# Token tiles of 128 rows with a last one of 113 instead of five of 125, rows of tokens at a pitch of 640 columns

## The chip, the core and the metric

The kernel runs on one core of a Trainium2 chip. The metric is the device time of one execution in microseconds (us); the times shown are medians of several runs. The core has five engines that work side by side from queues of their own: TensorE (PE, with its weight loads shown apart as PEld), VectorE (DVE), ScalarE (ACT), GpSimd (POOL) and SyncE (SP, which here only issues DMAs). The data moves through 16 DMA engines.

## The reference

The input is x, 625 tokens (graph nodes) by 1024 features in float32, and 20000 edges (src, dst), sorted by dst. The kernel computes

```
xn  = layernorm(x)
deg = number of edges into each node;  inv = 1 / max(deg, 1)
h   = relu(xn @ Ws0 + (segment_sum(xn[src], dst) * inv) @ Wn0 + b0)
g   = h @ Ws1 + (segment_sum(h[src], dst) * inv) @ Wn1 + b1
q,k,v = xn @ Wq, xn @ Wk, xn @ Wv           # 16 heads of 64
q   = softmax(q over features) / 8;  k = softmax(k over tokens)
m   = (q @ (k.T @ v) per head) @ Wo + bo
x   = x + g + m
y   = layernorm(x);  top 2 of 8 experts by softmax(y @ router_w)
x   = x + sum over the two of p_e * (silu(y @ w1[e]) @ w2[e])
        + sigmoid(y @ sgw) * ((silu(gate) * up) @ shared_down),  gate,up = y @ shared_gate_up
```

All weight matrices are 1024 x 1024 in float32 (shared_gate_up is 1024 x 2048). The result is x, 625 x 1024 float32.

## The kernel before

Every float32 operand is split into a high part in fp32r (`split`, L75: ACT casts, DVE or POOL subtracts) and a low part, and each product is three fp32r matmuls: high by high, high by low, low by high. Weights come as 512 KB pieces through one ordered `Stream` (SP issues the loads at L100, three buffers deep, six in the expert stage) and are split on arrival.

Tokens are cut into NT = 5 tiles of T = 125 rows. Two layouts occur. In the natural one the tokens lie on the partitions (`slot_n`: 128 x 5 x 1024), and one tile fills 125 of them. In the turned one the features lie on the partitions and the tokens along the row (`slot_t`: 128 x 8 x 626, so a row of tokens has a pitch of NP = 626 columns).

There are two kinds of products. `ws_tile` and `keys_step` keep the weights in the array (128 x 128) and stream the tokens past them in two stretches of about 313 columns. `ts_half` keeps one tile of tokens in the array (128 x 125) and streams 512 columns of weights past it:

```python
for t in range(NT):
    c = slice(t * T, (t + 1) * T)
    for k in range(2):
        kt = 2 * u + k
        ...
        nc.tensor.matmul(accs[t][:T, :], xh[:, kt, c], wh[:, k, :], start=f, stop=False)
        nc.tensor.matmul(accs[t][:T, :], xh[:, kt, c], wl[:, k, :], start=False, stop=False)
        nc.tensor.matmul(accs[t][:T, :], xl[:, kt, c], wh[:, k, :], start=False, stop=s)
```

One call is 120 matmuls (4 pieces of weights, 5 tiles, 2 k, 3 products), and it is called 14 times: queries (psq), values (psv), the output projection (pso), the neighbour products of both graph layers (psg, twice), the self product of the second (psx) and the shared expert's down projection (psz), two halves each. Within one piece of weights the tile is the outer loop, so six matmuls of one tile stand together.

The order of the stages:

1. Start. SP issues the loads of x tiles 0 and 1 (`load_x`, L282), the edges (L287), the first piece of Wk, x tiles 2 to 4, and then the stream. Each x tile is normalised in place (DVE statistics at L229, ACT or DVE at L305 and L307), turned on PE (L257) and split into xnh and xnl. ACT casts the edges (L313) and PE turns them (L317) so that 125 edges lie on the partitions.
2. Keys and the first self product: `keys_step` for 16 column blocks. The first three blocks are worked in two passes: first tokens 0 to 249 (x tiles 0 and 1), then, when tiles 2 to 4 are turned, the remaining columns.
3. Beside stage 2, the adjacency counts: DVE makes pairs of one-hot rows from 125 edges each (L432, L433), and PE multiplies them (L455). Each count is packed as one of five base-32 fields of a float, a field for each of the five token tiles of src. The inputs of the one-hots come from a chain on POOL (L414 to L424). The last link, `first_col`, is read by DVE into registers, ten times (`value_load`, L457). Then the counts are unpacked into ath, five tiles of tokens by 626 columns.
4. Queries, values, attention, output projection; graph layers 1 and 2; the second layer norm.
5. The shared expert's gate and up products, the router, a scatter of the tokens to expert rows (indirect DMA on POOL, L1050), eight experts with fixed capacities, a gather of the expert rows (indirect DMA on POOL, L1206).
6. End. The shared down projection (psz); for each of two halves and five tiles DVE adds the last product (L1217) and SP stores 125 rows of 512 columns (L1218).

A scheduler places the instructions of an engine's queue by priorities and estimated times, except where `keep_in_program_order` or `high_priority` binds them. The places of the one-hots and of the register loads in the DVE queue are its choice.

Of the kernel before, what the change touches and what calls it, by code (L numbers as in the profile page):

```python
# [20 lines left out]
T = 125  # L21
NT = N // T
NP = N + 1
D = 1024
KT = D // 128
E = 20000
NG = 10
CH = E // (T * NG)
# [19 lines left out]

@with_exitstack
def gps_layer(ctx: ExitStack, tc: tile.TileContext, x, src, dst,  # L50
# [12 lines left out]
    def slot_t(name, dt=F32R):  # L63
        t = big.tile([128, KT, NP], dt, name=name, tag="big")
        return t
# [109 lines left out]
    def ts_half(xh, xl, accs, first=True, last=True, step=None):  # L175
        for u in range(4):
            wh, wl = st.next()
            for t in range(NT):
                c = slice(t * T, (t + 1) * T)
                for k in range(2):  # L180
                    kt = 2 * u + k
                    f = first and kt == 0
                    s = last and kt == KT - 1
                    nc.tensor.matmul(accs[t][:T, :], xh[:, kt, c], wh[:, k, :], start=f, stop=False)  # L184
                    nc.tensor.matmul(accs[t][:T, :], xh[:, kt, c], wl[:, k, :], start=False, stop=False)  # L185
                    nc.tensor.matmul(accs[t][:T, :], xl[:, kt, c], wh[:, k, :], start=False, stop=s)  # L186
            if step:
                step(u)
# [35 lines left out]
    def stats(xt, mv, half=None, order=None):  # L224

        st6 = half if half is not None else small.tile([128, 2, 6], F32, name="bnst")
        for h in range(2):
            if half is None:
                order(nc.vector.bn_stats(st6[:T, h, :], xt[:, h * 512:(h + 1) * 512]))  # L229
        nc.vector.bn_aggr(mv, st6[:T])  # L230
# [21 lines left out]
    def to_t(nat, t, hi, lo, order=None):  # L252
        for g in range(2):
            ps = bank("pst").rearrange("p (a b) -> p a b", b=128)
            for k in range(4):
                kt = 4 * g + k
                tr = nc.tensor.transpose(ps[:, k, :T], nat[:, kt], ident[:T, :T])  # L257
                if order:
                    order(tr)
            done = split(ps[:, :, :T], hi[:, 4 * g:4 * g + 4, t * T:(t + 1) * T],  # L260
                         lo[:, 4 * g:4 * g + 4, t * T:(t + 1) * T])
# [15 lines left out]
    ei = big.tile([128, 2, CH * T], I32, name="ei", tag="big")  # L277
# [3 lines left out]
    def load_x(t):  # L281
        keep(nc.sync.dma_start(xts[:T, t, :], x[t * T:(t + 1) * T, :]))  # L282
# [8 lines left out]

    lnv = const.tile([128, NT, 2], F32, name="lnv")
    lnt = const.tile([128, 3, NT], F32, name="lnt")

    def first_stats(t):
        stats(xts[:T, t, :], lnv[:T, t, :], order=keep)

    def first_norm(a, b):
# [3 lines left out]
        for t in range(a, b):  # L302
            xt = xts[:T, t, :]
            if t % 2:
                nc.scalar.activation(xt, xt, AF.Identity, bias=z[:, t:t + 1], scale=y[:, t:t + 1])  # L305
            else:
                nc.vector.tensor_scalar(xt, xt, lnv[:T, t, 0:1], y[:, t:t + 1], op0=ALU.subtract, op1=ALU.mult)  # L307

    def first_turn(t, order=None):
        return to_t(xts[:T, t, :].rearrange("p (k c) -> p k c", c=128), t, xnh, xnl, order)  # L310

    edges = big.tile([128, 2, CH * T], F32, name="edges", tag="big")
# [3 lines left out]
    for i in range(2 * CH):  # L316
        nc.tensor.transpose(pse[:T, i, :], edges[:NG, i // CH, (i % CH) * T:(i % CH + 1) * T], ident[:NG, :NG])  # L317
    nc.scalar.copy(edt[:T], pse[:T])
    esrc, edst = edt[:T, :CH, :], edt[:T, CH:, :]
# [23 lines left out]
    def keys_back(o):  # L343
        ke = kbuf[:, o % 3, :N]
        for t0, n in ((0, 3), (3, 2)):
            ps = bank("pskt").rearrange("p (a b) -> p a b", b=128)
            for t in range(n):
                nc.tensor.transpose(ps[:T, t, :], ke[:, (t0 + t) * T:(t0 + t + 1) * T], ident)
            nc.scalar.copy(knat[:T, t0:t0 + n, o * 128:(o + 1) * 128], ps[:T, :n, :])
# [64 lines left out]
    keep(nc.gpsimd.tensor_scalar(field[:T], esrc, 1.0 / T, -0.496, op0=ALU.mult, op1=ALU.add))  # L414
    keep(nc.gpsimd.tensor_scalar(field[:T], field[:T], MAGIC, None, op0=ALU.add))
    keep(nc.gpsimd.tensor_scalar(field[:T], field[:T], MAGIC, None, op0=ALU.subtract))
    keep(nc.gpsimd.tensor_scalar(srow[:T], field[:T], -float(T), None, op0=ALU.mult))
    keep(nc.gpsimd.tensor_add(srow[:T], srow[:T], esrc))

    keep(nc.gpsimd.tensor_scalar(unit[:T], field[:T], BITS * 2.0 ** 23, (127.0 - 2 * BITS) * 2.0 ** 23,  # L420
                                 op0=ALU.mult, op1=ALU.add))
    keep(nc.gpsimd.tensor_sub(edst, edst, first_dst[:T, None, :].to_broadcast([T, CH, NG])))
# [8 lines left out]
    def one_hot(h, i, g):  # L431
        nc.vector.tensor_scalar(h[:T, :WIN], iota[:T, :WIN], edst[:, i, g:g + 1], None, op0=ALU.is_equal)  # L432
        nc.vector.tensor_scalar(h[:T, WIN:], iota[:T, :WIN], srow[:T, i, g:g + 1],  # L433
                                unit[:T, i, g:g + 1].bitcast(F32), op0=ALU.is_equal, op1=ALU.mult)
# [10 lines left out]
    def count_chunks(n):  # L445
        for _ in range(n):
# [7 lines left out]
            h = hot[:T, c % RING, :]  # L454
# [26 lines left out]
    ath = atp.tile([128, NT, NP], F32R, name="ath")  # L481
    degs = const.tile([128, 5, NT], F32, name="degs")
    two = const.tile([128, 2], F32R, name="two")
    nc.vector.memset(two.bitcast(F32), 1.0)

    def unpack():
        for s in range(NT - 1, 0, -1):
# [3 lines left out]
            nc.vector.tensor_scalar(ath[:T, s, :], part[:T], MAGIC, None, op0=ALU.subtract)  # L491
            nc.vector.scalar_tensor_tensor(packed[:T, :NP], ath[:T, s, :].bitcast(F32), -step, packed[:T, :NP],
                                           op0=ALU.mult, op1=ALU.add)
        nc.scalar.activation(ath[:T, 0, :], packed[:T, :NP], AF.Identity, scale=2.0 ** (2 * BITS))
        nc.vector.reduce_max(degs[:T, 4, 1:2], ath[:T, NT - 1, :].bitcast(F32), axis=AX.X)
# [5 lines left out]
    def degrees():  # L501
        ps = bank("psdg")
        for t in range(NT):
            for s in range(NT):
                nc.tensor.matmul(ps[:T, 2 * t:2 * t + 2], ath[:T, s, t * T:(t + 1) * T], two[:T],
                                 start=s == 0, stop=s == NT - 1)
        nc.vector.tensor_copy(degs[:T, 0, :], ps[:T, :2 * NT].rearrange("p (t k) -> p t k", k=2)[:, :, 0])
# [20 lines left out]
    def recount():  # L528
# [4 lines left out]
        nc.vector.tensor_tensor(edst, edst, first_dst[:T, None, :].to_broadcast([T, CH, NG]), op=ALU.add)  # L533
        nc.vector.tensor_scalar(field[:T], esrc, float(HW), None, op0=ALU.is_ge)
        nc.vector.scalar_tensor_tensor(esrc, field[:T], -float(HW), esrc, op0=ALU.mult, op1=ALU.add)
        nc.vector.tensor_scalar(field[:T], field[:T], 4095.0, 1.0, op0=ALU.mult, op1=ALU.add)
        with tc.For_i(0, NT, 1) as r:
            nc.vector.memset(acc, 0.0)
            with tc.For_i(0, NG, 1) as g:
                ps = bank("pa")  # L540
                for i in range(CH):
                    h = tmp.tile([128, WIN + HW + 1], F16, name="hrare", tag="tmp")
                    nc.vector.tensor_scalar(h[:T, :WIN], iota[:T, :WIN], edst[:, i, ds(g, 1)], None, op0=ALU.is_equal)
                    nc.vector.tensor_scalar(h[:T, WIN:WIN + HW], iota[:T, :HW], esrc[:, i, ds(g, 1)],
                                            field[:T, i, ds(g, 1)], op0=ALU.is_equal, op1=ALU.mult)
                    nc.tensor.matmul(ps[:, :HW], h[:T, :WIN], h[:T, WIN:WIN + HW], start=i == 0, stop=i == CH - 1)
# [7 lines left out]
        for j in range(NT):  # L554
            aj = tmp.tile([128, NP], F32, name="aj", tag="tmp")
            nc.gpsimd.dma_start(aj[:T], ard[j * T:(j + 1) * T, :])
            for s0, n in ((0, 3), (3, 2)):
                ps = bank("psat").rearrange("p (a b) -> p a b", b=128)
                for s in range(n):
                    nc.tensor.transpose(ps[:T, s, :T], aj[:T, (s0 + s) * T:(s0 + s + 1) * T], ident[:T, :T])  # L560
                c = slice(j * T, (j + 1) * T)
                al = tmp.tile([128, 3, T], F32R, name="al", tag="tmp")
                split(ps[:T, :n, :T], ath[:T, s0:s0 + n, c], al[:T, :n, :])
                for s in range(n):
                    nc.gpsimd.dma_start(atd[(s0 + s) * T:(s0 + s + 1) * T, c], al[:T, s, :])
        for t in range(NT):
            pt = bank("psdt")
            for s in range(NT):
                al = tmp.tile([128, T + 1], F32R, name="al", tag="tmp")
                nc.gpsimd.dma_start(al[:T, :T], atd[s * T:(s + 1) * T, t * T:(t + 1) * T])  # L570
                nc.tensor.matmul(pt[:T, :2], ath[:T, s, t * T:(t + 1) * T], two[:T], start=s == 0, stop=False)
                nc.tensor.matmul(pt[:T, :2], al[:T, :T], two[:T], start=False, stop=s == NT - 1)
            nc.vector.tensor_copy(degs[:T, 0, t:t + 1], pt[:T, 0:1])
        inverse_degrees()

    def low_part(s):
        al = tmp.tile([128, NP], F32R, name="al", tag="tmp")
        nc.gpsimd.dma_start(al[:T, :N], atd[s * T:(s + 1) * T, :N])
        nc.vector.memset(al[:T, N:NP].bitcast(F32), 0.0)
# [3 lines left out]
    def inverse(t0, n):  # L583
        ps = bank("psd").rearrange("p (a b) -> p a b", b=128)
        for t in range(n):
            nc.tensor.transpose(ps[:, t, :T], degs[:T, 2, t0 + t:t0 + t + 1].to_broadcast([T, 128]), ident[:T, :T])
        nc.scalar.copy(dinv[:, t0 * T:(t0 + n) * T].rearrange("p (a b) -> p a b", b=T), ps[:, :n, :T])
# [22 lines left out]
    def queries_back(half, t, q):  # L610
        qf = q.rearrange("p h d -> p (h d)")
        pt = bank("psqt").rearrange("p (a b) -> p a b", b=128)
        for k in range(4):
            nc.tensor.transpose(pt[:, k, :T], qf[:T, k * 128:(k + 1) * 128], ident[:T, :T])
        nc.scalar.copy(qt[:, 4 * half:4 * half + 4, t * T:(t + 1) * T], pt[:, :, :T])

    def queries(half, accs):
        for t in range(NT):
            ps = accs[t][:T, :].rearrange("p (h d) -> p h d", d=64)
# [629 lines left out]
```

## Time and profile before

| | us |
|---|---|
| median of 3 runs | 1074.67 (1072.81 to 1074.84) |
| the profiled execution's own time | 1069.91 |
| its span from first to last instruction | 1068.3 |
| PE busy in the span | 1021.3 |
| DVE / ACT / POOL busy | 600.7 / 395.4 / 172.0 |
| mean granted TensorE clock | 0.984 |
| matmuls of 128 x 125 by 512 columns, one group of 80, busy time | 31.5 to 32.6 |
| DMA moved | 164.30 MB, mean 154 GB/s |

The profile gives each engine's busy time, the groups of instructions, what each wait was ended by, and the timeline. A matmul's own duration overlaps its successor's, so the pace of PE is read from the distance between starts, not from durations. The DMA share is the mean busy share of all 16 DMA engines, so one engine that is always busy counts 1/16.

### The profile page before, as it was taken

The page shows a single profiled execution, that of the slowest core. Times are in us where ns is not written, and L with a number is a line of the kernel's source. Part 1 is how long each engine was busy: PE and PEld are TensorE (multiplying, and loading weights), DVE is VectorE, ACT ScalarE, POOL GpSimd, SP SyncE. Part 2 cuts the span into 40 slices and gives each one's busy share as a digit, 9 for nine tenths or more (in the row PEclk, how much of TensorE's full clock was granted, in tenths as well). Part 3 has the DMA queues.
Part 4 walks back from the last instruction along what each step waited for, and adds up shares of the span by engine and source line. Part 5 has one row for each costly group of instructions (what it writes and reads, how often), then busy time and mean ns, then how long its engine had stood idle before and what let it go on. Part 6 is the DMA issues. An engine that isn't in the chain of part 4 may idle for free. (4 is left out here: it accounts for less than half of the span.)

```text
span 1068.3 us, 14752 instructions
## 1 busy us (share of the span) xinstructions
PE 1021.3 (96%) x5571; PEld 872.7 (82%) x5571; DVE 600.7 (56%) x1188; ACT 395.4 (37%) x577; POOL 172.0 (16%) x204
## 2 busy tenths in 40 slices
PE   4789999999999999999999999999999989999986
PEld 2689999888887777977777899998878777887765
DVE  2599953545253322722326636258686788877481
ACT  2333423222231122222113432246656576776410
POOL 2322001211015300010000104123030033200310
PEclk7899999999999999999999999999999999999999
DMA  5222134666233522052221125866967898888961
GB/s 134 87 60 61 41 96 143 216 231 223 62 119 115 165 88 79 23 154 79 73 68 38 31 60 131 237 193 193 277 233 231 263 300 282 281 286 269 305 152 73
DMA packets 116344, 164.30 MB, mean 154 GB/s; under 512 B 11079, under 2 KB 68431, under 8 KB 116262
## 3 DMA queue, kind: packets, MB, share of 16 engines
q1 hardware_dynamic: 97606, 118.54, 35.2%
q0 software_dynamic: 18656, 44.71, 14.1%
q8 instruction: 47, 0.77, 0.3%
q14 instruction: 35, 0.29, 0.1%
HBM read 133.04 MB, written 30.16 MB: 153 GB/s over the span
## 5 line engine op out<-in xcount | busy, mean ns | idle before, releaser
L75 DVE TENSOR_TENSOR wlo<-wraw,whi 128x1024 fp32r<-128x1024 f32 x140 | 177.9, 1271 | 267.4 <-ACT whi L75 266.4
L75 ACT CAST whi<-wraw 128x1024 fp32r<-128x1024 f32 x149 | 156.3, 1049 | 306.2 <-PE psg L186 68.2
L1089 PE MATMUL pse<-xs,whi 128*128 128x448 f32 (+1 forms) x384 | 108.9, 357 | 0.0
L75 DVE TENSOR_TENSOR wlo<-wmore,whi 128x1024 fp32r<-128x1024 f32 x67 | 86.9, 1297 | 23.5 <-ACT whi L75 22.5
L1085 PE MATMUL pse<-xs,wlo 128*128 128x224 f32 (+1 forms) x384 | 89.6, 254 | 0.6 <-DVE wlo L75 0.6
L75 ACT CAST whi<-wmore 128x1024 fp32r<-128x1024 f32 x67 | 70.3, 1049 | 51.6 <-PE psz L186 22.4
L376 PE MATMUL psk<-xnh,whi 128*128 128x314 f32 (+3 forms) x256 | 83.9, 328 | 4.8 <-DVE xnl L75 4.5
L377 PE MATMUL psk<-xnl,whi 128*128 128x314 f32 (+3 forms) x256 | 79.6, 311 | 1.0 <-DVE xnl L75 0.9
L378 PE MATMUL psk<-xnh,wlo 128*128 128x314 f32 (+3 forms) x256 | 79.5, 310 | 0.0
L1085 PEld LDWEIGHTS pse<-xs,wlo 128*128 128x128 f32 x384 | 72.0, 190 | 1.7 <-DVE wlo L75 0.8
L1141 PE MATMUL psy<-wlo,he 128*128 128x512 f32 (+1 forms) x176 | 70.0, 397 | 3.3 <-DVE wlo L75 3.0
L1089 PEld LDWEIGHTS pse<-xs,whi 128*128 128x128 f32 x384 | 69.0, 189 | 2.4
L1140 PE MATMUL psy<-whi,he 128*128 128x512 f32 (+1 forms) x176 | 69.5, 395 | 0.0
L1142 PE MATMUL psy<-whi,he 128*128 128x512 f32 (+1 forms) x176 | 69.0, 392 | 0.0
L433 DVE TENSOR_SCALAR hot<-iota,srow,unit 125x128 f16<-125x128 f16 x160 | 56.6, 354 | 0.0
L376 PEld LDWEIGHTS psk<-xnh,whi 128*128 128x128 f32 x256 | 49.4, 193 | 5.8 <-DVE xnl L75 5.0
L75 POOL TENSOR_TENSOR xs<-raw,xs 128x512 fp32r<-128x512 f32 (+2 forms) x24 | 34.4, 1455 | 104.2 <-ACT xs L75 83.4
L377 PEld LDWEIGHTS psk<-xnl,whi 128*128 128x128 f32 x256 | 49.3, 193 | 1.4 <-DVE xnl L75 1.4
L378 PEld LDWEIGHTS psk<-xnh,wlo 128*128 128x128 f32 x256 | 49.0, 192 | 0.1
L432 DVE TENSOR_SCALAR hot<-iota,edt 125x128 f16<-125x128 f16 x160 | 43.7, 273 | 7.9 <-issue 7.9
L1141 PEld LDWEIGHTS psy<-wlo,he 128*128 128x128 f32 (+1 forms) x176 | 31.8, 180 | 14.8 <-DVE wlo L75 6.7
L1140 PEld LDWEIGHTS psy<-whi,he 128*128 128x128 f32 (+1 forms) x176 | 31.9, 181 | 10.1
(337 smaller groups left out, 2385.0 us busy)
## 6 DMA issues: line engine op xcount, KB each, us to landing
wraw<-in_L_ffn_w_dram SPq DMA_DIRECT2D x65, 512.0 KB
wmore<-in_L_ffn_w_dram SPq DMA_DIRECT2D x63, 512.0 KB
xsd<-zt POOLq DMA_DIRECT2D x9, 1024.0 KB, 6.2
wraw<-in_L_gnn_W_self_dram SPq DMA_DIRECT2D x16, 512.0 KB
wraw<-in_L_gnn_W_neigh_dram SPq DMA_DIRECT2D x16, 512.0 KB
wraw<-_ffn_shared_gate_up_dram SPq DMA_DIRECT2D x16, 512.0 KB
wraw<-in_L_mix_Wk_dram SPq DMA_DIRECT2D x8, 512.0 KB
wraw<-in_L_mix_Wq_dram SPq DMA_DIRECT2D x8, 512.0 KB
```

What stands on the lines that cost most here:

```text
L75: return (nc.scalar.copy(hi, srcap), (eng or nc.vector).tensor_sub(lo, srcap, hi.bitcast(F32)))
L376: nc.tensor.matmul(ps[:, :n], wh[:, kt, :], xnh[:, kt, c], start=kt == 0, stop=False)
L377: nc.tensor.matmul(ps[:, :n], wh[:, kt, :], xnl[:, kt, c], start=False, stop=False)
L378: nc.tensor.matmul(ps[:, :n], wl[:, kt, :], xnh[:, kt, c], start=False, stop=kt == KT - 1)
L432: nc.vector.tensor_scalar(h[:T, :WIN], iota[:T, :WIN], edst[:, i, g:g + 1], None, op0=ALU.is_equal)
L433: nc.vector.tensor_scalar(h[:T, WIN:], iota[:T, :WIN], srow[:T, i, g:g + 1], unit[:T, i, g:g + 1].bitcast(F32), op0=ALU.is_equal, op1=ALU. ...
L1085: nc.tensor.matmul(ps[a][:, :n], wl[:, k, c], xs[:, kt, 0, :], start=False, stop=False)
L1089: nc.tensor.matmul(ps[a][:, :2 * n], wh[:, k, c], xs[:, kt], start=kt == 0, stop=kt == KT - 1)
L1140: nc.tensor.matmul(acc, h(kt, 0), wh[:, k, :], start=kt == 0, stop=False)
L1141: nc.tensor.matmul(acc, h(kt, 0), wl[:, k, :], start=False, stop=False)
L1142: nc.tensor.matmul(acc, h(kt, 1), wh[:, k, :], start=False, stop=kt == KT - 1)
```

## The change

T becomes 128, so the tiles have 128, 128, 128, 128 and 113 rows. `rows(t)` and `cols(t)` give the partitions and columns of tile t, and every place that used `[:T]` and `t * T` uses them. The edges keep their own 125 (ET). Rows of tokens in the turned layout, and those of ath, get a pitch of XP = 640 columns instead of 626. Loads of x and stores of the result go through `pieces(t)`, which cuts the last tile into 112 rows and 1 row, so SP issues one load more and two stores more. The two stretches of the shared products become 384 and 242 columns (they were 374 and 252), and those of the first three key blocks 256 and 370 (they were 250 and 376). Three small memsets (lnv, degs, lgt) fill the rows that the last tile doesn't write, and the degrees are copied in two instructions. The branch for rare graphs (`recount`) is changed too; it isn't taken with these inputs.

```diff
 N = 625
-T = 125
-NT = N // T
+T = 128
+NT = -(-N // T)
...
+XP = NT * T
...
-CH = E // (T * NG)
+ET = 125
+CH = E // (ET * NG)
...
+def rows(t):
+
+    return slice(0, min(T, N - t * T))
+
+
+def cols(t):
+
+    return slice(t * T, min((t + 1) * T, N))
+
+
+def pieces(t):
+
+    n = min(T, N - t * T)
+    m = n // 16 * 16
+    return [(slice(t * T + a, t * T + b), slice(a, b)) for a, b in ((0, m), (m, n)) if b > a]
...
-        t = big.tile([128, KT, NP], dt, name=name, tag="big")
+        t = big.tile([128, KT, XP], dt, name=name, tag="big")
...
-                c = slice(t * T, (t + 1) * T)
+                c, acc = cols(t), accs[t][rows(t), :]
...
-                    nc.tensor.matmul(accs[t][:T, :], xh[:, kt, c], wh[:, k, :], start=f, stop=False)
...
+                    nc.tensor.matmul(acc, xh[:, kt, c], wh[:, k, :], start=f, stop=False)
...
-                tr = nc.tensor.transpose(ps[:, k, :T], nat[:, kt], ident[:T, :T])
+                tr = nc.tensor.transpose(ps[:, k, rows(t)], nat[:, kt], ident[rows(t), rows(t)])
...
     def load_x(t):
-        keep(nc.sync.dma_start(xts[:T, t, :], x[t * T:(t + 1) * T, :]))
+        for r, p in pieces(t):
+            keep(nc.sync.dma_start(xts[p, t, :], x[r, :]))
...
+    nc.vector.memset(lnv, 1.0)
...
-        for t0, n in ((0, 3), (3, 2)):
+        for t0, n in ((0, NT - 1), (NT - 1, 1)):
...
-    ath = atp.tile([128, NT, NP], F32R, name="ath")
+    ath = atp.tile([128, NT, XP], F32R, name="ath")
     degs = const.tile([128, 5, NT], F32, name="degs")
+    nc.gpsimd.memset(degs, 0.0)
...
-        nc.vector.tensor_copy(degs[:T, 0, :], ps[:T, :2 * NT].rearrange("p (t k) -> p t k", k=2)[:, :, 0])
+        for a, b in ((0, NT - 1), (NT - 1, NT)):
+            nc.vector.tensor_copy(degs[rows(a), 0, a:b],
+                                  ps[rows(a), 2 * a:2 * b].rearrange("p (t k) -> p t k", k=2)[:, :, 0])
...
-            nc.gpsimd.dma_start(xr[:T], x[t * T:(t + 1) * T, hs])
...
+            nc.gpsimd.dma_start(xr[p], x[cols(t), hs])
...
-                nc.tensor.matmul(accs[t][h][:T, :], a[:T, s, t * T:(t + 1) * T], g[:T, s, h * 512:(h + 1) * 512],
+                nc.tensor.matmul(accs[t][h][rows(t), :], a[rows(s), s, cols(t)], g[rows(s), s, h * 512:(h + 1) * 512],
                                  start=start, stop=stop)
...
-    lgt = late.tile([20, NP], F32, name="lgt")
+    lgt = late.tile([20, XP], F32, name="lgt")
+    nc.gpsimd.memset(lgt[:, NP:], 0.0)
...
-    SPARTS = ((0, 3 * T - 1), (3 * T - 1, NP - 3 * T + 1))
+    SPARTS = ((0, 3 * T), (3 * T, NP - 3 * T))
...
-                        out=xsd[:, :], out_offset=bass.IndirectOffsetOnAxis(ap=slot[k][:T, t:t + 1], axis=0),
-                        in_=xfn[:T, t, :], in_offset=None)
+                        out=xsd[:, :], out_offset=bass.IndirectOffsetOnAxis(ap=slot[k][rows(t), t:t + 1], axis=0),
+                        in_=xfn[rows(t), t, :], in_offset=None)
...
-                out=ys[k][:T, t, :], out_offset=None, in_=ysd[:, :],
-                in_offset=bass.IndirectOffsetOnAxis(ap=slot[k][:T, t:t + 1], axis=0))
+                out=ys[k][rows(t), t, :], out_offset=None, in_=ysd[:, :],
+                in_offset=bass.IndirectOffsetOnAxis(ap=slot[k][rows(t), t:t + 1], axis=0))
...
-            nc.sync.dma_start(out[t * T:(t + 1) * T, hs], o)
+            for r, p in pieces(t):
+                nc.sync.dma_start(out[r, hs], x2[p, t, hs])
```

## The prediction

> **What bounds the kernel now.** I read the page first, then the sums by window, then the timeline where PE is idle.
>
> ```profile
> span 1068.3 us, 14752 instructions
> ...
> PE 1021.3 (96%) x5571; PEld 872.7 (82%) x5571; DVE 600.7 (56%) x1188; ACT 395.4 (37%) x577; POOL 172.0 (16%) x204
> ...
> PE   4789999999999999999999999999999989999986
> PEclk7899999999999999999999999999999999999999
> DMA  5222134666233522052221125866967898888961
> ```
>
> PE is the bound from the third slice (one is 26.7 us) to the last but one. There a change counts by the time between two starts of matmuls. In the first two slices and in the last one PE waits or is done, and other chains decide. So there are three places to cost: PE's pace, the start, the end.
>
> PE's pace, from the timeline: one stretch with 125 columns in the array, one with 128.
>
> ```profile
> 387.16 0.40 PE L186 MATMUL psg<-whi,xnl 128*125 128x512 f32 x1
> ...
> 389.49 0.39 PE L184 MATMUL psg<-whi,xnh 128*125 128x512 f32 x1
> ```
> ```profile
> 846.14 0.39 PE L1142 MATMUL pse<-whi,xs 128*128 128x512 f32 x1
> ...
> 847.96 0.39 PE L1141 MATMUL pse<-wlo,xs 128*128 128x512 f32 x1
> ```
>
> Between the first two lie 10 starts, 2.33 us, 233 ns each; between the second two 8 starts, 1.82 us, 227 ns each. Both stream 512 columns at the full clock, and the printed durations (0.39 to 0.40) hide the difference. Over all six sets of 125 columns outside psz the distance has a mean of about 232.4 ns.
>
> The start and the end, by window (columns: busy time of PE, PEld, DVE, ACT, POOL, then clock, DMA share, GB/s):
>
> ```profile
> 9.00:12.00 3.00, 0.00 (x0) 0.00 (x0) 1.49 (x3) 0.00 (x0) 0.00 (x0) 1.00 0.33 134
> 1004.00:1007.00 3.00, 3.00 (x15) 2.39 (x14) 0.00 (x0) 0.00 (x0) 2.39 (x3) 1.00 1.07 399
> 1061.00:1066.00 5.00, 0.00 (x0) 0.00 (x0) 0.00 (x0) 0.00 (x0) 0.00 (x0) 0.84 0.33 127
> ```
>
> While x is loaded and while the result is stored, DMA runs at a third of its share: five engines of 16 are busy, 125 = 5 x 25 rows. With all 16 the chip moved 399 GB/s. Each of the five carries 134/5, about 26 GB/s.
>
> What waits for this at the start (timeline):
>
> ```profile
> 13.23 1.29 DVE L229 BATCH_NORM_STATS2 bnst<-xts 125x6 f32<-125x512 f32 x2 [2.59 <-DMA xts<-in_x_dram]
> 17.56 3.51 ACT L313 CAST edges<-ei 10x4000 f32<-10x4000 int32 x1
> 21.22 6.86 PE L317 MATMUL psed<-ident,edges 10*125 10x10 f32 x32 [12.92 <-ACT edges L313]
> 31.54 0.58 PE L376 MATMUL psk<-xnh,whi 128*128 128x250 f32 x1
> ```
>
> It is one chain: x tile 1 lands (13.23), statistics, ACT's normalisation, ACT's cast of the edges, their transposes, those of x, the first key product at 31.54. And the second hole of PE, 46.7 to 54:
>
> ```profile
> 42.95 0.19 POOL L424 CAST first_col<-first_dst 1x10 int32<-1x10 f32 x1
> ```
> ```profile
> 49.28 0.26 DVE L432 TENSOR_SCALAR hot<-iota,edt 125x128 f16<-125x128 f16 x1 [7.93 <-issue]
> 50.88 3.02 DVE L75 TENSOR_TENSOR xnl<-pst,xnh 128x500 fp32r<-128x500 f32 x5
> ```
>
> DVE's queue holds eight register loads of first_col (L457) ahead of the first one-hot. They wait for POOL's 43.14 and then take until 49.28, 0.77 us each. Behind them stand the splits xnl that PE needs; the last ends at 54.55.
>
> **The change, part by part.** The sum is made against the profiled execution, 1069.91 us (span 1068.3); the median of the runs is 4.76 above it.
>
> *Start, loads.* SP's loads of x go from 5 engines to 16. Tiles 0 and 1 are 1.05 MB: 7.8 us at 134 GB/s, 2.6 at 399. Tile 1's load is issued by 1.7, and start and landing take some 2.5 (an estimate: its 7.6 us of data, with edges and a share of Wk on the same five engines, ended at 13.2). So it lands at about 6.5 instead of 13.2: 6.7 earlier. If the reads get only 250 GB/s it is 4.9; it can't be above 8. All that follows is in chains without another wait for DMA: the edges (160 KB) and Wk's first piece (needed at ACT's 20.98) stand behind x in the same queue and speed up with it; x tiles 2 to 4 end near 12 to 16, needed by 22. L313, L317, L257, POOL's wlo splits and L414 to L424 move as a block. The last tile's extra load of one row costs SP 0.4 us at about 4 us, when nobody waits for SP. The lnv memset (0.07 us, DVE at 1.4) lies before the first data; those of degs and lgt (each under 0.3) lie in POOL's idle time at 3 and 596.
>
> *Start, DVE's order.* In the changed program's instruction order DVE has, after L307: two pairs of one-hots, two xnl splits, two pairs, three register loads, two splits, b0t, two splits. The other seven loads come later. From POOL's end of L424 I sum 0.78 + 1.26 + 0.78 + 3 x 0.77 + 1.26 + 0.15 + 1.26 = 7.8 us, where before it was 54.55 - 43.14 = 11.4. That is 3.7 less on the chain to PE. The seven moved loads cost DVE 5.4 us later, between about 80 and 110, where DVE is busy all the time; but there the one-hots are made 13 us or more ahead of the matmul that uses them (for example made at 102.4, used at 115.5), and the maxima L354 feed transposes some 7 us later. So I cost them at nothing; without that cover they would take back up to 5.4. PE's wait of 2.1 us at 76 to 78 (for L354 behind the one-hots) moves along. Together 10.4 us. Bounds: 5 (slow reads, the order worth little) to 15 (the clock also holds, next paragraph).
>
> *The clock in the start.* The page "TensorE: Matmul & The Clock Gate" of the Trainium skill (Part 1, the HAM clock gate) says that an idle window of about 3.4 us halves the clock and that windows run free of the kernel. The row: PE idles from 8.3 to 21.2, L317 takes 210 ns a transpose, and the windows show a granted clock of 0.50 for 25 to 29. The hole shrinks to about 6 us. If the trace's chain is just moved, L317 keeps its 6.86; by the rule a 6 us hole need not hold a whole idle window, and then L317 and L257 halve, 5 us more. A hole of 6 us holds one in about 3 of 4 cases, so I keep the trace's value and put the 5 us into the low end.
>
> *PE's pace.* 14 halves of 120 matmuls in `ts_half`. 120 of them, psz's first half, end in a wait for the gather and gain nothing: 1560 are left, and 100 of psm. After the change, of each 30 four tiles (24) have 128 columns and one (6) has 113. The trace's mixed stretches (128 beside 96 or 64 columns) show the first five or so of a run of 128 still at about 231.7 and then 226.7, and 96 columns at about 232. So a group of 30 has (5 x 231.7 + 19 x 226.7 + 6 x 232) / 30 = 228.6, 3.8 ns less. 1560 x 3.8 = 5.9, psm about 0.4: 6 us. Here the same page speaks against the change (section "Back-to-back issue gap"): the gap is N/2.4 + 2.5 ns by the streamed columns alone, 215.7 for 512, and a load of P columns takes P/1.2 beside it (section "LDWEIGHTS"), so 125 or 128 in the array is the same, and the term would be 0. The trace shows 233 against 227 for the same N, so I take the trace; 0 stays the upper bound of the time, 7.6 us of gain (all 24 at once at 226.7) the lower. That the 6 ns come from the columns and not from the pitch or the layout is a reading of two layouts, not a test.
>
> *Streams past the weights.* 314 and 312 columns stay; 374 + 252 become 384 + 242, 250 + 376 become 256 + 370: same sums, 0. DVE, ACT and PSUM work on up to 128 partitions at the same row length, and the tiles' total length stays (4 x 125 becomes 4 x 128, four times, and 4 x 113 once): 0. The second copy of the degrees is some 0.2 us of DVE, which then is waited for by nobody.
>
> *POOL's queue.* xr, accd, x2, scatter and gather keep their number and bytes. Here 125 rows already run on nearly all engines (share 0.98 to 1.07 in the gather). Costed 0; see the third rival.
>
> *End.* The last L1217 ends at 1060.28, the span at 1068.3: five stores of 256 KB at 127 GB/s take 10 us, and DVE hands over a tile each 1.4 us.
>
> ```profile
> 1059.53 0.75 DVE L1217 SCALAR_TENSOR_TENSOR x<-psz,sg,x 125x512 f32<-125x512 f32 x1 [0.64 <-PE psz L186]
> ```
>
> With 16 engines a store takes 0.7 us, so none queues. What remains after DVE is start 0.8 (first store: 1054.73 to 1055.5), 0.4 for the second issue of the last tile, 0.2 to 0.7 of data and 1.7 to the span's end: 3.1 instead of 8.0, 4.9 less (4.2 to 5.5).
>
> Sum: 10.4 + 6.0 + 4.9 = 21.3. The profiled execution would be 1048.6, the median 1074.67 - 21.3 = 1053.4.
>
> **The rivals.**
> 1. PE's pace follows the page, or the jitter is of the layout's making: the 6 us are missing, 1059. For it: the rule; and 128 columns beside 96 pace like 96. Against: the steady 227 of whole stretches.
> 2. The start doesn't carry through: ACT's cast, the POOL chain or the DMA of Wk becomes the new wait, or DVE falls behind with its later loads. Then 4 instead of 10.4, 1060; with the first rival too, 1066. For it: DVE is full from 64 to 110. Against: the 13 us of lead.
> 3. The last tile's 113 rows fall on one engine in POOL's queue. The page "DMA: Bandwidth & Descriptors" (section "Why a DMA increments its semaphore by 16 and not by 1") states that the number of engines is the largest up to 16 that divides the rows, so a prime number gets one, with an exception for some of POOL's copies. `pieces` is used on SP's queue only. Place: the two scatters and two gathers of tile 4. 226 rows of 4 KB at 26 GB/s take 36 us; the gather would land near 1054 instead of 1033, 21 us of PE's wait, and the scatter near 703 instead of 687, which eats the 9 us that the first expert's input is early and costs 7 more. 28 - 21.3 = 7 slower, 1081. It decides as soon as tile 4's gather takes over 20 us more than its share. Against: 125 rows show a share near 1 there, where the rule's 5 engines would show 0.33.
>
> **How the numbers follow.** Likeliest as summed 0.63; first rival 0.18; second 0.13; third 0.05; the rest unknown. Low end: 15 + 7.6 + 5.5 gives 28, 1046.6; the half clock that a window at 214:218 shows may go too (1.7 us): 1045. High end: the second rival with its spread, 1063; the third and the double case stay out. A measurement of this kernel can tell about 0.2% from no change, 2.1 us; faster by more 0.94, within 0.01, slower 0.05.
>
> **What would show it.** Right: L229 of tile 1 starts near 6 to 7, the first key product near 24 to 25, the last early split near 44; DMA share over 0.6 while x loads; starts of psg 227 apart within the first four tiles; the span ends 3 us after the last L1217. Wrong: starts of 232 in tiles of 128 columns; new waits of PE for L354 or the one-hots at 60 to 110; a gather that lands less than 28 us before the end (35 now); a wait of the first expert for xs.

## The result and the profile after

The changed kernel takes 1059.33 us (median of 4 runs, 1056.29 to 1062.61); the kernel before took 1074.76 beside it on the same chip (1072.81 to 1075.71). The ratio is 0.986, with a 95% interval of 0.983 to 0.989: 15.4 us less, where 21.3 were forecast. The profiled execution of the changed kernel took 1056.29 us, 3.0 below its median.

First the page of the changed kernel: busy times, then the row of PE, of the granted clock and of the bytes moved, in 40 slices of 26.4 us.

```profile
span 1054.3 us, 14764 instructions
...
PE 1010.2 (96%) x5571; PEld 870.8 (83%) x5571; DVE 601.1 (57%) x1190; ACT 394.9 (37%) x577; POOL 175.0 (17%) x206
...
PE   6889999999999999999999999999999899999958
...
PEclk7999999999999999999999999999999999999979
...
GB/s 183 42 80 52 70 81 205 223 217 175 81 110 172 134 76 66 111 72 76 80 81 2 44 78 250 140 221 217 247 261 236 281 306 284 272 256 308 313 50 82
```

PE's first slice went from 4 to 6 and its last from 6 to 8. But the last slice but one fell from 8 to 5, the clock has a 7 there, and the DMA moved only 50 GB/s. That is new. From the timeline, the starts of PE at these places make a ledger (us from the span's start):

| stage ends where | before | after | moved by | in this stage |
|---|---|---|---|---|
| last set of keys starts | 155.3 | 144.0 | -11.3 | -11.3 start |
| psz starts | 999.9 | 980.5 | -19.4 | -8.1, mostly pace |
| its last matmul ahead of the wait starts | 1031.9 | 1011.6 | -20.2 | -0.8 pace |
| psz goes on | 1035.1 | 1025.0 | -10.1 | **+10.1 wait** |
| last addition of L1217 / L1249 ends | 1060.3 | 1050.8 | -9.5 | +0.6 |
| span ends | 1068.3 | 1054.3 | -14.0 | -4.5 end |

The -8.1 is a net figure: matched matmul by matmul, PE was 20.4 us ahead at 690 and lost 1.0 of it among the experts, to causes that are not shown.

The start, in the timeline after: tile 1's statistics, the cast of the edges, their transposes, the first key product; then DVE's first one-hot and the last two early splits.

```profile
7.24 1.29 DVE L248 BATCH_NORM_STATS2 bnst<-xts 128x6 f32<-128x512 f32 x2 [1.06 <-DMA xts<-in_x_dram]
11.57 3.51 ACT L334 CAST edges<-ei 10x4000 f32<-10x4000 int32 x1
15.23 6.86 PE L338 MATMUL psed<-ident,edges 10*125 10x10 f32 x32 [7.85 <-ACT edges L334]
25.62 0.38 PE L398 MATMUL psk<-xnh,whi 128*128 128x256 f32 x1 [0.22 <-ACT xnh L94]
...
36.73 0.26 DVE L454 TENSOR_SCALAR hot<-iota,edt 125x128 f16<-125x128 f16 x1 [1.66 <-POOL edt L444]
...
43.04 1.15 DVE L94 TENSOR_TENSOR xnl<-pst,xnh 128x452 fp32r<-128x452 f32 x2
```

The chain is 6.0 us early at 7.24 (13.23 before) and 5.9 at the first key product (31.54 before). DVE's first one-hot now follows POOL's chain at once (1.66 of waiting instead of 7.93), so the last early split ends at 44.2 and not at 54.55. The cast of the edges keeps its duration, and the edges' transposes still take 6.86, at half clock. Behind the second hole the clock differs too. Windows behind PE's restart, before and after:

```profile
54.00:56.00 2.00, 2.00 (x7) 2.00 (x8) 2.00 (x9) 0.00 (x0) 0.00 (x0) 0.50 0.00 0
44.00:46.00 2.00, 2.00 (x13) 2.00 (x13) 2.00 (x11) 0.00 (x0) 0.00 (x0) 1.00 0.00 0
```

(Columns as in the prediction: PE, PEld, DVE, ACT, POOL, clock, DMA share, GB/s.) Before, PE waited 4.5 us in one piece for the splits and restarted at half clock (0.50), up to about 57; after, no wait there is above 0.8 us and PE restarts at full clock. That is worth 1.7 us: PE is 10.2 us ahead at its restart and 12.0 by 64.

PE's pace, one stretch that goes over from 128 columns to 113:

```profile
380.01 0.39 PE L203 MATMUL psg<-whi,xnh 128*128 128x512 f32 x1
...
382.05 0.39 PE L203 MATMUL psg<-whi,xnh 128*113 128x512 f32 x1
...
383.41 0.39 PE L203 MATMUL psg<-whi,xnh 128*128 128x512 f32 x1
...
384.77 0.39 PE L203 MATMUL psg<-whi,xnh 128*128 128x512 f32 x1
```

Nine starts in 2.04 us, six in 1.36, six in 1.36: 227 ns each, with 113 columns as with 128. Before it was 233.

Now windows of the changed kernel, with the same columns: the loads of x, the gather of tiles 0 to 3, the gather of tile 4, the stores; then the gather of the kernel before. (A window counts packets by their starts, so its share can pass 1.)

```profile
8.00:12.00 4.00, 0.00 (x0) 0.00 (x0) 2.61 (x10) 1.77 (x3) 0.00 (x0) 0.90 1.11 356
987.00:998.00 11.00, 11.00 (x50) 9.04 (x49) 7.25 (x11) 2.10 (x2) 8.87 (x8) 1.00 0.99 359
1006.00:1016.00 10.00, 6.02 (x27) 4.59 (x25) 0.00 (x0) 1.05 (x1) 0.00 (x0) 0.94 0.13 53
1047.00:1052.00 5.00, 2.98 (x14) 2.05 (x12) 2.25 (x3) 0.00 (x0) 0.00 (x0) 1.00 0.49 177
```
```profile
1009.00:1031.00 22.00, 22.00 (x96) 17.50 (x95) 13.26 (x18) 3.15 (x3) 7.98 (x7) 1.00 0.94 222
```

The share is near 1 in both kernels' gathers, but several transfers are in flight there. Where the first one has just begun they differ: with 128 rows the traces have a share of 0.98 and 336 GB/s (988 to 988.5), with 125 rows in the kernel before 133 GB/s (1007.5 to 1008.5), which is five times one engine's 26.5. Later, too, 125 rows moved less at the same share (222 GB/s against 359): their packets of 4 KB took 257 ns on the mean, those of 128 rows 180. Why they are longer is not shown.

From 1006 to 1016 the share is 0.13, which is two engines of 16, at 26.5 GB/s each: tile 4's two gathers, 113 rows each, on one engine each. When one of the two has landed, the share is 0.06 (1019 to 1022). DVE, in the timeline, waits for them, and PE waits for DVE. The third block is PE at the same place in the kernel before.

```profile
1000.40 3.39 DVE L1248 SCALAR_TENSOR_TENSOR x<-ys,top,x 128x512 f32<-128x512 f32 x5
1018.54 1.41 DVE L1248 SCALAR_TENSOR_TENSOR x<-ys,top,x 113x512 f32<-113x512 f32 x2 [14.74 <-DMA ys<-ysd,slot]
1022.82 1.41 DVE L1248 SCALAR_TENSOR_TENSOR x<-ys,top,x 113x512 f32<-113x512 f32 x2 [2.87 <-DMA ys<-ysd,slot]
1024.15 0.74 DVE L1249 SCALAR_TENSOR_TENSOR x<-psz,sg,x 128x512 f32<-128x512 f32 x1
```
```profile
1007.56 0.39 PE L205 MATMUL psz<-whi,stl 128*113 128x512 f32 x1
1007.78 0.39 PE L203 MATMUL psz<-whi,sth 128*128 128x512 f32 x1
...
1011.64 0.39 PE L205 MATMUL psz<-whi,stl 128*128 128x512 f32 x1
1024.95 0.80 PE L203 MATMUL psz<-whi,sth 128*128 128x512 f32 x1 [12.93 <-DVE x L1249]
1025.54 0.63 PE L204 MATMUL psz<-wlo,sth 128*128 128x512 f32 x1
```
```profile
1031.86 0.39 PE L186 MATMUL psz<-whi,stl 128*125 128x512 f32 x1
1035.09 0.49 PE L184 MATMUL psz<-whi,sth 128*125 128x512 f32 x1 [2.84 <-DVE x L1217]
```

psz's first half ends at 1007.6, with the 113 columns of tile 4, and the second half starts at once. The kernel has eight PSUM banks (`bufs=8`), and the first half holds five of them until the additions of L1249 have read them, so three tiles of the second half, 18 matmuls, can run. The fourth tile waits. DVE's queue is in order, and L1248 of tile 4 stands ahead of the first L1249, which frees the bank. So the wait is 13.3 us from start to start (3.2 before, at the same place). And the hole costs twice: the clock falls to half in it, and the matmuls behind it, to 1028.4, start 427 ns apart (0.63 instead of 0.39 each), 1.7 us more.

### The profile page after: what moved, and what is told of

It reads as the page before. It is cut to its first block, busy times and chain, and to the rows that moved or that the text cites. A ratio compares the mean times of both kernels' runs of the same rounds, so it can differ in the third digit from the quotient of the medians.

```text
span 1054.3 us, 14764 instructions
## 1 busy us (share of the span) xinstructions
PE 1010.2 (96%) x5571; PEld 870.8 (83%) x5571; DVE 601.1 (57%) x1190; ACT 394.9 (37%) x577; POOL 175.0 (17%) x206
## 5 line engine op out<-in xcount | busy, mean ns | idle before, releaser
L94 DVE TENSOR_TENSOR wlo<-wmore,whi 128x1024 fp32r<-128x1024 f32 x67 | 86.9, 1297 | 26.3 <-ACT whi L94 25.3
L1173 PE MATMUL psy<-whi,he 128*128 128x512 f32 (+1 forms) x176 | 69.1, 392 | 0.0
L203 PE MATMUL psz<-whi,sth 128*128 128x512 f32 (+1 forms) x80 | 32.1, 401 | 14.4 <-DVE x L1249 12.9
```

Of the source, the lines that this page charges most:

```text
L94: return (nc.scalar.copy(hi, srcap), (eng or nc.vector).tensor_sub(lo, srcap, hi.bitcast(F32)))
L203: nc.tensor.matmul(acc, xh[:, kt, c], wh[:, k, :], start=f, stop=False)
L1173: nc.tensor.matmul(acc, h(kt, 1), wh[:, k, :], start=False, stop=kt == KT - 1)
```

## The experiments

**The gather of tile 4 in two pieces** (g64), and **the scatter as well** (gs64). Tile 4's rows go as 0 to 63 and 64 to 112; the indices of the second piece are copied to the start of a small tile of their own. Other tiles stay whole.

```
+            tail = [rt(f"tail{k}", 1, dt=I32) for k in range(2)]
...
                 nc.vector.tensor_copy(slot[k][:T], slf[:T])
+                nc.vector.tensor_copy(tail[k][:49], slot[k][64:113, NT - 1:])
...
+    if t < NT - 1:
+        return ((slice(0, T), slot[:T, t:t + 1]),)
+    return ((slice(0, 64), slot[:64, t:t + 1]), (slice(64, 113), tail[:49]))
...
-            nc.gpsimd.indirect_dma_start(
-                out=ys[k][rows(t), t, :], out_offset=None, in_=ysd[:, :],
-                in_offset=bass.IndirectOffsetOnAxis(ap=slot[k][rows(t), t:t + 1], axis=0))
+            for p, i in parts(t, slot[k], tail[k]):
+                nc.gpsimd.indirect_dma_start(
+                    out=ys[k][p, t, :], out_offset=None, in_=ysd[:, :],
+                    in_offset=bass.IndirectOffsetOnAxis(ap=i, axis=0))
```

> Edit to the kernel after the change: only the gather of tile 4 is issued as two indirect DMAs, of 64 and of 49 rows, instead of one of 113 rows. Theory A (113 is prime, so each of tile 4's two gathers runs on a single DMA engine): 49 = 7 x 7 and 64 = 4 x 16 rows spread, the packets of 4096 B end near 1001 instead of 1022, PE's gap of 13.3 us before psz's second half falls below 1.5 us and the stretch at half clock behind it (1.7 us) is gone: 13 to 15 us less than the kernel after the change, about 1045, 0.973 of the kernel before. Theory B (the gather is late for another reason, POOL's longer issues of 2.4 and 3.5 us or the queue's total bytes): the gap stays above 9 us, 1056 to 1060.

> As g64, and the scatter of tile 4 in two pieces of 64 and 49 rows as well. Theory A: the scatter's last 4096 B packet lands near 652 instead of 671, the first xb load is issued some 15 us earlier, but PE is busy until 692 with the router's last weights, so the time is that of g64 within 2 us. Rival: the first expert's input was what set 692; then 5 us or more below g64.

g64: 1043.08 us, 0.969 of the kernel before (0.965 to 0.973); the change alone has 0.983 to 0.989, so the intervals are apart. The span falls from 1054.3 to 1038.5. Windows of g64 (the gather of whole tiles, then of the last pieces), DVE at the border of psz's halves, and PE where it had waited:

```profile
988.00:998.00 10.00, 10.00 (x46) 8.21 (x45) 8.21 (x12) 1.06 (x1) 7.73 (x8) 1.00 1.02 408
1001.00:1003.00 2.00, 2.00 (x11) 1.65 (x10) 2.00 (x4) 0.24 (x1) 0.00 (x0) 1.00 0.45 137
```
```profile
1004.09 1.21 DVE L101 TENSOR_TENSOR wlo<-wmore,whi 128x1024 fp32r<-128x1024 f32 x1
1005.23 1.39 DVE L1259 SCALAR_TENSOR_TENSOR x<-psz,sg,x 128x512 f32<-128x512 f32 x2
1006.55 0.73 DVE L1258 SCALAR_TENSOR_TENSOR x<-ys,top,x 113x512 f32<-113x512 f32 x1
```
```profile
1010.63 0.39 PE L212 MATMUL psz<-whi,stl 128*128 128x512 f32 x1
1010.86 0.39 PE L210 MATMUL psz<-whi,sth 128*128 128x512 f32 x1
```

Tile 4's rows are there before DVE asks, on some 7 engines (0.45 x 16; 49 is 7 x 7). PE goes on to the fourth tile of psz's second half in 0.23 us, and the clock stays full. Also the 3.2 us that the kernel before waited here are gone. The theory holds, and with 15.8 us of span it is worth a little more than expected.

gs64: 1041.43 us, 0.967 (0.962 to 0.973), the same as g64. The first xb load is issued at 660.9 instead of 676.4, so the scatter too was late by 15 us in the change, but PE is busy with the shared expert until 692 either way. A transfer that is 15 us late cost nothing there, and in the gather 10.

**The gather of tile 4 first** (gfirst), nothing split:

```
-    for t in range(NT):
+    for t in (NT - 1, *range(NT - 1)):
         for k in range(2):
             nc.gpsimd.indirect_dma_start(
```

> Edit to the kernel after the change: the gathers of tile 4 (113 rows) are issued ahead of those of the other tiles, not behind them. Nothing is split. Theory A (113 rows on one engine each, 113 x 0.16 = 18 to 21 us whatever else is in the queue): they land at about 1005 to 1008, under the 16-engine gathers of the others, before psz's first half ends at 1011; PE's gap falls under 3 us, and the time is within 3 us of g64 (0.969 to 0.973). Rival (what is issued last is late because of the queue): now tile 3 is late and the gap stays at 9 us or more.

Not as theory A expected: 1063.99 us, 0.988 (0.981 to 0.994). A window of gfirst, then its DVE and its POOL (timeline):

```profile
1012.00:1016.00 4.00, 0.00 (x0) 0.00 (x0) 0.00 (x0) 0.00 (x0) 0.00 (x0) 0.50 0.13 53
```
```profile
1018.05 1.42 DVE L1248 SCALAR_TENSOR_TENSOR x<-ys,top,x 113x512 f32<-113x512 f32 x2 [30.67 <-DMA ys<-ysd,slot]
1020.14 0.75 DVE L1248 SCALAR_TENSOR_TENSOR x<-ys,top,x 113x512 f32<-113x512 f32 x1 [0.68 <-DMA ys<-ysd,slot]
1020.81 1.22 DVE L94 TENSOR_TENSOR wlo<-wmore,whi 128x1024 fp32r<-128x1024 f32 x1
```
```profile
1002.73 0.94 POOL L1237 DMA_INDIRECT ys<-ysd,slot  x1 [0.30 <-issue]
1018.29 1.33 POOL L1237 DMA_INDIRECT ys<-ysd,slot  x1 [14.62 <-DMA ys<-ysd,slot]
```

The two gathers of 113 rows again keep two engines alone at the end (0.13), so their slowness goes with their rows and not with their place in the queue. But on an engine that also carries its share of the other gathers they need from 994 to 1018, not the 18 us of 113 packets alone (0.159 us each), and the order moved DVE's wait: DVE now stands for 30.7 us at tile 4, with the split wlo behind it that PE needs for the last piece of weights of psz's first half. PE's hole moved there (15.2 us) instead of closing. POOL's last two gathers were issued only when the slow ones had ended.

**The pitch, the columns and the block's start** (p626, c125, b640, p632). Each but c125 changes one number in `slot_t`: p626 as shown, p632 to 632, b640 from NP to 640 in the kernel before. c125 uses 125 columns of a tile for the three products, but for the first and the last of a sum.

```
-        t = big.tile([128, KT, XP], dt, name=name, tag="big")
+        t = big.tile([128, KT, NP], dt, name=name, tag="big")
```
```
+                    m = min(acc.shape[0], 125)
+                    n, d = acc[:m], slice(c.start, c.start + m)
...
-                    nc.tensor.matmul(acc, xh[:, kt, c], wl[:, k, :], start=False, stop=False)
+                    nc.tensor.matmul(n, xh[:, kt, d], wl[:, k, :], start=False, stop=False)
```

> Edit to the kernel after the change: the activation tiles keep tiles of 128 and 113 rows but get back the pitch of 626 columns (one line). Layout theory (the start of a stationary block in memory sets the pace): ts_half's matmuls start 231 to 233 ns apart again instead of 227, about 1560 x 5.5 ns = 8.6 us more than the kernel after, near 1068, 0.994 of before. Column theory (the one of the prediction: 128 columns in the array pace at 227): four tiles of five stay at 227, within 2 us of the kernel after.

> Edit to the kernel after the change: in ts_half only 125 of the 128 columns of a tile are used as the stationary block (but for the first and the last matmul of a tile's sum); the three rows left out lack most of their sums. Layout theory: the starts stay 226 to 227 ns apart. Column theory: the matmuls with 125 columns start 231 to 233 ns apart.

> Edit to the kernel before: only the pitch of the activation tiles goes from 626 to 640 columns; tiles of 125 columns, at multiples of 125 as before. If the pitch alone lets PE settle into the 227 ns rhythm, its sets show 227 in their later groups, some 7 to 9 us less. If the start of each block inside the row matters as well (125 x 4 bytes is no multiple of 64), 231 to 233 stays.

> Edit to the kernel after the change: pitch of 632 columns (2528 bytes, a multiple of 32 and not of 64) instead of 640. If 32 bytes are enough, every set stays at 227; if 64 are needed, half of the blocks start off it and the starts are 229 to 233 ns apart, as with 626.

Distances of starts in ts_half, worked out from the starts of about 1300 matmuls of each trace:

| kernel | columns | pitch | block starts at | mean distance |
|---|---|---|---|---|
| before | 125 | 626 | 125 t | 232.6 |
| b640 | 125 | 640 | 125 t | 232 |
| p632 | 128, 113 | 632 | 128 t | 232 |
| p626 | 128, 113 | 626 | 128 t | 231.0 |
| c125 | 125, 113 | 640 | 128 t | 231 to 233 or 227 |
| after, g64 | 128, 113 | 640 | 128 t | 226.7 |

With 128 columns and the old pitch (p626) the slow pace is back, and with a pitch of 632 as well; with the new pitch and the old starts (b640) it stays. So one of the two alone is not enough, and a pitch of a multiple of 32 bytes is not either (632 x 4 = 79 x 32). p626 took 1063.39 us, 0.988 (0.983 to 0.993), which by time alone can't be told from the change: 1560 x 4.3 = 6.7 us of pace are lost (8.6 were expected), but PE's wait for the gather shrinks by 2.3 (11.0 instead of 13.3). b640 took 1071.09 and p632 1058.61, single runs that tell nothing of a few us; their traces do.

c125 fits neither theory. It has two rhythms, each steady, in one set of sums (timeline; in the second stretch six matmuls of 113 columns lie between the lines shown):

```profile
455.15 0.39 PE L206 MATMUL psg<-wlo,hth 128*125 128x512 f32 x1
...
457.25 0.39 PE L206 MATMUL psg<-wlo,hth 128*125 128x512 f32 x1
```
```profile
470.35 0.39 PE L206 MATMUL psg<-wlo,hth 128*125 128x512 f32 x1
...
473.07 0.39 PE L206 MATMUL psg<-wlo,hth 128*125 128x512 f32 x1
```

Nine starts in 2.10 us, 233 ns each; 15 us later twelve in 2.72, 227 each. The three starts of a group take 700 or 680 ns. After a pause c125 stays in the slow rhythm for up to 120 matmuls and then drops into the fast one and keeps it to the next pause; the change does so within some fifteen; before, p626, p632 and b640 never do. So 125 columns are not what makes a start slow. They make the fast rhythm harder to get into, and the other pitches and starts that were tried keep it out. Whether starts and pitch at multiples of 64, 128 or 256 bytes would do was not tried; why the layout matters is open.

**The start and the end without the middle** (bsp), and **DVE's order on top** (bspo), both on the kernel before:

```
+    def pieces(t):
+        return [(slice(t * T + a, t * T + b), slice(a, b)) for a, b in ((0, 112), (112, T))]
...
-        keep(nc.sync.dma_start(xts[:T, t, :], x[t * T:(t + 1) * T, :]))
+        for r, p in pieces(t):
+            keep(nc.sync.dma_start(xts[p, t, :], x[r, :]))
...
-            nc.sync.dma_start(out[t * T:(t + 1) * T, hs], o)
+            for r, p in pieces(t):
+                nc.sync.dma_start(out[r, hs], x2[p, t, hs])
```
The second edit, bspo's:

```
+                with tc.issue_after(last[0].ins), tc.issue_after(last[1].ins):
                     first_v = nc.vector.value_load(first_col[0:1, g:g + 1], min_val=0, max_val=N - 1)
```

> Edit to the kernel before: tiles stay at 125 rows and the pitch at 626, but each load of x and each store of the output goes out as two DMAs of 112 and 13 rows (112 = 16 x 7, 13 rows on 13 engines). It should have the start and the end of the change without its middle. Theory (rows per DMA decide how many engines carry it): statistics of x tile 1 start near 7.2 (13.2 before), the first key product near 25.6, the first set of queries near 204 to 206, PE's pace stays at 232, and the span ends 3.5 us after the last addition instead of 8.0: 14 to 16 us less than the kernel before, 0.985 to 0.987. Rival (the gain at the start and the end comes from the tiles of 128 rows themselves): 0.997 to 1.

> bsp (kernel before with loads and stores in 112 + 13 rows), and DVE's register loads of first_col are kept behind the early splits of x (one with-line, the order alone). bsp's first key product came 5.3 us earlier than before, but PE's restart after its second hole only 3.8, since DVE read registers for 5 us ahead of the splits. Theory (the start is two terms, the loads and DVE's order, and the second decides how much of the first arrives): the last early split ends near 44, PE's restart near 43.5 to 45 instead of 50.2, the wait at 76 moves to 68 to 70, and the time is 5 to 7 us below bsp, about 1059, 0.985 of before. Rival (the order costs nothing on the path, something else ate bsp's start): within 2 us of bsp.

bsp took 1065.48 us, 0.991 (0.988 to 0.994): faster, but by some 9 us and not 15. bspo took 1059.69, 0.984 (0.978 to 0.990), as expected. PE's times in the start:

| | first key product | restart after the second hole | after the wait for exp | psa starts |
|---|---|---|---|---|
| before | 31.5 | 54.0 | 78.4 | 307.0 |
| bsp | 26.3 | 50.2 | 75.7 | 307.3 |
| bspo | 27.0 | 44.6 | 69.1 | 297.7 |
| after | 25.6 | 43.7 | 67.3 | 293.3 |

DVE in bsp and in bspo (timeline), the early splits:

```profile
47.09 3.02 DVE L75 TENSOR_TENSOR xnl<-pst,xnh 128x500 fp32r<-128x500 f32 x5 [4.98 <-issue]
```
```profile
41.56 3.01 DVE L75 TENSOR_TENSOR xnl<-pst,xnh 128x500 fp32r<-128x500 f32 x5
```

In bsp DVE idles 5 us ahead of the splits for no release that the profile shows. The trace has its register loads there: the ten start from 39.4 to 46.4, about 0.65 us apart at the end. In bspo they start from 70.2 on, and PE restarts 5.5 us earlier. The times of the two runs alone show it less well, since their intervals touch. In the profiled execution of bsp (1069.57, 4.1 above its median) all that was left of the start was lost by 307 us, to longer stretches at half clock: its windows beside those of before (which waits for exp up to 78.4).

```profile
76.00:80.00 4.00, 4.00 (x22) 3.81 (x21) 4.00 (x11) 1.20 (x2) 2.36 (x1) 0.57 0.02 4
213.00:220.00 7.00, 7.00 (x20) 5.60 (x20) 3.36 (x14) 0.00 (x0) 0.85 (x2) 0.51 0.81 290
```
```profile
76.00:80.00 4.00, 1.86 (x17) 1.68 (x16) 4.00 (x19) 2.48 (x5) 0.28 (x1) 1.00 0.00 0
213.00:220.00 7.00, 7.00 (x33) 5.85 (x33) 4.03 (x16) 0.82 (x2) 0.42 (x2) 0.76 0.79 260
```

At 213 to 220 bsp starts 20 matmuls where before starts 33. The end came as forecast in both: 3.4 and 3.3 us from the last addition to the span's end. So bspo, with tiles of 125 rows and no gain of pace, reaches the time of the change: it has most of the start and the end, and no gather of 113 rows.

**The best of both** (g64o): g64 with the same line for the register loads.

> g64 (after, gather of tile 4 in 64 + 49 rows) with the same line: here three register loads stand between the one-hots and the splits, 2.3 us of DVE. If they are on the path as the prediction summed, PE's restart at 42.9 moves to 41 to 42 and 1 to 2 us are won; if DVE waits for ACT's halves xnh there anyway, nothing (within 1 us of g64's 1043).

1039.05 us, 0.965 (0.960 to 0.971). PE's restart came at 41.9, but its wait for exp at 62 to 66 took 3.4 us, and at psa (293.2) it was no earlier than g64 (292.5). The spans are 1038.2 and 1038.5, and the intervals overlap: no difference from g64 can be told, though both beat the change and the kernel before.

## Why the prediction was right, and where it was not

The direction and the order of size were right, and the time, 5.9 us above the forecast, lies in its range. But the 0 for POOL's queue was wrong by about 12 us; some 4 of that were given back by a start and a pace that gained more than summed, and that is luck. The time alone would also fit the first two rivals (1059 and 1060), whose outcomes the trace rules out: the gain of pace is there, and the start carries through.

- *Start, loads, 6.7.* Right: 6.0 at the statistics, 5.9 at the key product. While x loads, the DMA share is 1.11, at 356 GB/s, where it was 0.33 at 134.
- *Start, DVE's order, 3.7* (its own terms make 3.6). Right: the restart came 10.2 early, 5.9 of it from the loads, so 4.3. bsp and bspo show that the term is real; without it 3.8 us of 5.2 arrived at the restart. The seven register loads that moved behind cost nothing, as costed: they start from 77.1 to 94.8, and PE loses nothing there.
- *The clock in the start.* The hole ahead of the edges' transposes was 7.9 us, not 6, and they stayed at half clock, as the trace's value had it. Not costed was PE's full clock behind the second hole, 1.7 us. Half of that went at the wait for exp, which grew from 2.4 to 3.2 because PE came to it early: the maximum that exp needs (L354, now L376) came 11.1 us earlier in DVE's full queue, and so did PE behind the wait. All in all the start gave 11.3 where 10.4 were summed.
- *PE's pace, 6.0.* Too small, by a wrong reading. Columns were taken to set the pace, so that 113 columns and the first five matmuls behind them stayed slow. In fact 113 columns pace at 226.7 in the new layout, and 128 columns at 231 in the old one (p626). The ledger has 8.1 us net to psz and 0.8 up to its wait, 8.9. The prediction had called the reading untested; p626 and p632 decide against it, with b640 for the starts. That a gain came all the same is luck: the change happened to set pitch and starts as well. The rule that it was weighed against (the Trainium skill, "TensorE: Matmul & The Clock Gate", section "Back-to-back issue gap": 215.7 ns for 512 columns) fits neither rhythm; 226.7 and 233.3 were measured, so the first rival's 0 is out, though its other reading, that the layout makes the pace, is what the runs show. The section gives that formula for an isolated matmul, and about 131 ns for a stream with weight loads, which no run here comes near. The weight loads don't explain the rhythms: they show 188, 185 and 175 ns for 128, 125 and 113 columns in every layout.
- *End, 4.9.* Right: 4.5 (8.0 became 3.5).
- *POOL's queue, 0.* This step failed. The third rival named mechanism and place, tile 4's gather on one engine; it was given 0.05 since 125 rows show a DMA share near 1 in the gather, where five engines would show a third. That share is the sum of several gathers in flight: it says nothing about one. The trace of before had the answer at the start of its gather, 133 GB/s where 16 engines gave 399. The prediction also has PE wait at the end of psz's first half; the wait comes 18 matmuls later, so 138 matmuls and not 120 gain nothing, a matter of 0.1 us. The rule quoted from "DMA: Bandwidth & Descriptors" (section "Why a DMA increments its semaphore by 16 and not by 1") agrees with what the runs show for the gather of 113 rows (one engine each), of 49 (about seven) and of 128 (a share of 0.98 as the first one begins); no exception for POOL's indirect gathers is seen here.
- *The third rival's size.* It had 21 us for the gather and 7 for the scatter on top, 28; it cost 10.1 of wait and 1.7 of half clock. Two things were mis-sized: the two gathers of tile 4 ran on two engines side by side (0.13, not 0.06), and the late scatter had cover until 692.5 (gs64 against g64: no difference).
- *What would show it.* The marks at the start, of the pace and of the end came within 0.7 us of what was written. The mark for the gather, "lands less than 28 us before the end", did not strike, though the gather was the fault: the last landing at 1022.8 is 31.5 before the end. It was counted from the wrong place; what counts is when psz needs its next free bank, at 1011.6.

## What to carry to other kernels

Give each tile's DMA a number of rows with a large divisor up to 16, the last tile's too; it mattered here on SP's queue and for POOL's indirect gathers. A remainder that is prime goes in two pieces. A DMA share near 1 with several transfers in flight does not show that one of them is wide: look at the end of the group, where the last one is alone. And put the wait that a late transfer makes against the work that covers it: 15 us late cost nothing in the scatter and 10 in the gather.

## What the runs showed of the hardware that was not expected

- Matmuls of the same shape have two steady rhythms, 680 and 700 ns for three starts of 512 columns. Which one is taken depends on where the stationary block lies: at a pitch of 2560 bytes with starts at multiples of 512 PE falls into the faster one; at a pitch of 2528 or 2504 bytes, or with starts at multiples of 500, no stretch of 30 matmuls had its mean (the least was 229.2). The printed durations, 0.39 or 0.40 us in both, hardly show it; the distances of the starts do.
- Gathers of 128 rows, several in flight, moved 359 to 408 GB/s, those of 125 rows 222, and one of 113 rows 26.5.
- A hole in PE's work has a second price. The gap of 13.3 us brought 3.4 us at half clock behind it, and shorter holes in the start shift such stretches about: bsp's profiled execution lost 1.5 us of its head start at 76 to 80 and as much again at 213 to 220.
